# A new order of the work in each slot of an attention schedule, with another split of the PSUM banks

## Chip, cores and metric

The kernel runs on one core of one Trainium2 chip. The metric is device time in microseconds (us) of that core; "before" is the median of three runs.

## What is computed

One launch computes four residual layers over x, 8 batches of 256 × 512, all in fp32. The first two are attention, and they are what the change touches; the last two are scans over 256 time steps.

- Layer 0, masked attention: for each batch, q = xᵀ·Wqᵀ gives 512 tokens of 8 heads with 32 elements. Keys, queries and values are all q. Scores of masked keys are replaced by -1e30, rows of masked queries by zero; softmax, product with the values, output product with Wo, and x is added.
- Layer 1, modulated attention: RMS norm of x, scaled and shifted by a modulation that is computed from the condition (`emb @ W_emb + b_emb`); qkv product; RMS norm of q and k per head; softmax attention with 16 heads over 256 tokens; `o + o @ W_out`, and x is added.
- Layers 2 and 3: an oscillator integrated by four-stage Runge-Kutta steps and a GRU cell, both over 256 steps.

A softmax may be shifted by any number per query row; the kernel shifts by row maxima so that the exponentials stay in range.

## The kernel before

The engines are called PE (matmul), DVE (vector), ACT (scalar), POOL and SP (here the queue that issues every DMA). Each engine works through its own instructions strictly in program order, and the program order is written out by hand: `tc.manual_schedule()` with one loop over slots, g from -5 to 79 (lines 462 to 526). In each slot the loop calls one small step of several batches at once; a batch starts every U = 8 slots, so that a steady stretch repeats every eight slots (a "period"). The slots of a period are counted here as g mod 8, 0 to 7.

Layer 0 of a batch has two groups of four heads (e = 0, 1), each with four blocks of 128 keys (kc = 0 to 3), so eight blocks, one in each slot:

- `project` (line 170) makes q; DVE masks it into qm, ACT copies it; `project_out` (186) transposes the copy in the next slot.
- `scores0` (192): four matmuls, one for each head, into four PSUM banks, and four ACT copies into an SBUF block `sc`.
- `maxima0` (206): DVE's row maxima of a block, into `mxp0[e]`.
- `rows0` (212), once for each group, at the end of the slot of its fourth block: four PE transposes of `mxp0[e]`, an ACT copy, a DMA to DRAM (`row`) and a DMA that broadcasts the row to all partitions (`bc`, one buffer).
- `weights0` (224), five slots after the block's scores: DVE subtracts `bc` from the block, ACT exponentiates in place.
- `values0` (229), one slot later: eight matmuls, products with the values and with ones, accumulated over the four blocks in the banks c0 and c1. After the fourth, `weigh0` (246) divides on DVE and finishes on POOL.
- `masked_out` (260): output product and addition to x.

Layer 1 of a batch follows: `normalize` (273), `modulate` (285), six `qkv` products (300), one in each slot, with `qkv_norm` (323; DVE and POOL) and in the next slot `qkv_out` (337), which transposes q and k. Four head steps c = 0 to 3 then take one slot each:

- `maxima1` (346): sixteen matmuls into four banks, and four DVE maxima into `mxp1` (one buffer), which release the banks.
- one slot later `rows1` (362): transposes and an ACT copy `mrow`; `weights1` (369): scores again into four banks with the maxima subtracted by a matmul, and four ACT exponentials `ex`.
- one slot later `values1` (393): products into one more bank, `weigh` (162) on DVE.
- `modulated_out` (401) and, a slot later, `modulated_turn` (418), for each half of the tokens; its result goes out through SP (`x2d`).

For all but the last two batches a slot does one `qkv`; batches 6 and 7 do two. `modulation` (123) makes the scale and shift of all batches, once, in slot 4: 64 small matmuls, and the identity added to `wout_sb`.

[...] Everything but c0 and c1 takes its bank from one pool of six through `bank()` (lines 57 and 60). A tile that takes a bank over waits until the bank's last reader is done:

```python
ps_s = ctx.enter_context(tc.tile_pool(name="a_ps_s", bufs=6, space=PSUM))
ps_c = ctx.enter_context(tc.tile_pool(name="a_ps_c", bufs=1, space=PSUM))
...
def at(g, rel, n=1):
    b, r = divmod(g - rel, U)
    return (b, r) if 0 <= b < B and r < n else None
```

`at(g, -4, U)` names the block whose scores are made in slot g, `at(g, 1, U)` that of `weights0`, `at(g, 2, U)` that of `values0`. `heads(g, rel)` names the batch and head step in the same way.

Of the kernel before, what the change touches and what calls it, by code (L numbers as in the profile page):

```python
# [8 lines left out]
F32 = mybir.dt.float32  # L9
AF = mybir.ActivationFunctionType  # L10
ALU = mybir.AluOpType
AX = mybir.AxisListType
PSUM = bass.MemoryType.PSUM

P = 128
B, T, D = 8, 256, 512
NJ = D // P
# [7 lines left out]
def attention(ctx, tc, cst, x, cond, wqT, woT, w_emb, b_emb, g_norm, w_qkv, g_q, g_k, w_out, follow):  # L25
# [28 lines left out]
    first = ExitStack()  # L54
    fone = first.enter_context(tc.tile_pool(name="a_fone", bufs=1, side="right"))
    ftwo = first.enter_context(tc.tile_pool(name="a_ftwo", bufs=2, side="right"))
    ps_s = ctx.enter_context(tc.tile_pool(name="a_ps_s", bufs=6, space=PSUM))
    ps_c = ctx.enter_context(tc.tile_pool(name="a_ps_c", bufs=1, space=PSUM))

    def bank(shape, name):  # L60
        return ps_s.tile(shape, F32, tag="s", name=name)

    def line(name):
        return sm.tile([P, D], F32, tag="line", name=name, bufs=6)
# [14 lines left out]
    with tc.manual_schedule():  # L79
        nc.sync.dma_start(wq_sb, wqT.rearrange("(k p) e -> p k e", p=P))  # L80
        load(0)
        cst["rest"]()
        vec = wp.tile([12, P], F32, name="vec")
        nc.sync.dma_start(vec[0:8, :], b_emb.rearrange("(f p) -> f p", p=P))
        nc.sync.dma_start(vec[8:12, :], g_norm.rearrange("(f p) -> f p", p=P))
        gq_sb = wp.tile([P, 1], F32, name="gq_sb")
        gk_sb = wp.tile([P, 1], F32, name="gk_sb")
        for i in range(4):
            nc.sync.dma_start(gq_sb[32 * i : 32 * i + 32, :], g_q.unsqueeze(1))
            nc.sync.dma_start(gk_sb[32 * i : 32 * i + 32, :], g_k.unsqueeze(1))  # L90

        wemb = [
            two.tile([P, 2 * D], F32, tag=tag, name=f"wemb_{k}", bufs=bufs)
            for k, (tag, bufs) in enumerate((("qT", 1), ("kT", 1), ("vt", 2), ("vt", 2)))
        ]
        for k in range(NJ):
            nc.sync.dma_start(wemb[k], w_emb[k * P : (k + 1) * P, :])
        load(1)
        wo_sb = fone.tile([P, 2, 256], F32, name="wo_sb")
        nc.sync.dma_start(wo_sb, woT.rearrange("(k p) e -> p k e", p=P))  # L100
        wqkv_sb = wp.tile([P, NJ, 3 * D], F32, name="wqkv_sb")
        nc.sync.dma_start(wqkv_sb, w_qkv.rearrange("(k p) f -> p k f", p=P))
        wout_sb = wp.tile([P, NJ, D], F32, name="wout_sb")
        nc.sync.dma_start(wout_sb, w_out.rearrange("(k p) f -> p k f", p=P))

    gqs = wp.tile([P, 1], F32, name="gqs")
    mhalf = wp.tile([P, 16], F32, name="mhalf")
# [12 lines left out]
    vecT = wp.tile([P, 12], F32, name="vecT")  # L120
    ssT = wp.tile([P, 8, B], F32, name="ssT")

    def modulation():

        nc.vector.tensor_scalar_mul(gqs, gq_sb, SC)
        pv = bank([P, 28], "pvs")
        nc.tensor.transpose(pv, cst["vecs"], ident[0:28, 0:28])
        nc.vector.tensor_copy(cst["vecS"], pv)
        pv = bank([P, 12], "pv")
        nc.tensor.transpose(pv, vec, ident[0:12, 0:12])  # L130
        nc.vector.tensor_copy(vecT, pv)
        pe = bank([P, 8, B], "pe")
        for f in range(8):
            for k in range(NJ):
                nc.tensor.matmul(
                    pe[:, f, :],
                    lhsT=wemb[k][:, f * P : (f + 1) * P],
                    rhs=condT[:, k, :],
                    start=(k == 0),
                    stop=(k == NJ - 1),  # L140
                )
        nc.vector.tensor_tensor(ssT, pe, vecT[:, 0:8].unsqueeze(2).to_broadcast([P, 8, B]), ALU.add)
        nc.vector.tensor_scalar_add(G, ssT[:, 0:NJ, :], 1.0)
        nc.vector.tensor_tensor(G, G, vecT[:, 8:12].unsqueeze(2).to_broadcast([P, NJ, B]), ALU.mult)
        nc.vector.tensor_copy(shift, ssT[:, NJ:8, :])

        for c in range(NJ):
            nc.vector.tensor_add(wout_sb[:, c, c * P : (c + 1) * P], wout_sb[:, c, c * P : (c + 1) * P], ident)
# [75 lines left out]
    def weights0(b, e, kc):  # L224
        sc = scs[b, e, kc]
        nc.vector.tensor_sub(sc, sc, bcs[b, e])  # L226
        nc.scalar.activation(sc, sc, AF.Exp, bias=negT[:, kc, b : b + 1], scale=SC)  # L227

    def values0(b, e, kc):
        if kc == 0:  # L230
            if e == 0:
                ctxTs[b] = fone.tile([P, 2, D], F32, tag="ctxT", name=f"ctxT_{b}")
            pc0s[b, e] = [ps_c.tile([P, D], F32, tag=f"c{i}", name=f"pc0_{b}_{e}_{i}") for i in range(2)]
        sc = scs.pop((b, e, kc))
        for half in range(2):
            for h in range(4):
                o = e * P + h * DH
                nc.tensor.matmul(
                    pc0s[b, e][half][32 * h : 32 * h + 32, :],
                    lhsT=qtoks[b][:, kc, o : o + DH] if half == 0 else ones[:, 0:DH],  # L240
                    rhs=sc[:, h, :],
                    start=(kc == 0),
                    stop=(kc == NJ - 1),
                )
# [100 lines left out]

    def maxima1(b, c):
        qT, kT = qTs[b], kTs[b]
        ss = [bank([P, 2, 256], f"n1_{b}_{c}_{h}") for h in range(4)]
        for qc in range(2):
            for h in range(4):  # L350
                r = 32 * h
                nc.tensor.matmul(
                    ss[h][:, qc, :],
                    lhsT=qT[r : r + 32, c, qc * P : (qc + 1) * P],
                    rhs=kT[r : r + 32, c, :],
                    start=True,
                    stop=True,
                )
        for h in range(4):
            nc.vector.tensor_reduce(mxp1[:, :, 32 * h], ss[h], AX.X, ALU.max)  # L360
# [32 lines left out]
    def values1(b, c):  # L393
        if c == 0:
            oTs[b] = big.tile([P, NJ, 256], F32, tag="oT", name=f"oT_{b}")
        pc = bank([P, 2, 256], f"pc1_{b}_{c}")
        for half in range(2):
            values(pc, half, lambda k, h: vts[b][:, k, c * P + h * DH : c * P + (h + 1) * DH], [exs1[b, c]])
        weigh(pc, oTs[b][:, c, :], f"1_{b}_{c}")
# [44 lines left out]
    def at(g, rel, n=1):  # L444

        b, r = divmod(g - rel, U)
        return (b, r) if 0 <= b < B and r < n else None

    def heads(g, rel):

        for b in range(B):
            if 0 <= g - HEADS[b] - rel < NJ:
                return b, g - HEADS[b] - rel
        return None

    left = {}

    def leave(kind):
        for key in [k for k in left if k[0] == kind]:
            yield *key[1:], left.pop(key)  # L460

    with tc.manual_schedule():
        for g in range(-5, OUT[-1][1] + 2):

            if a := at(g, -4, U):
                scores0(a[0], a[1] // 4, a[1] % 4)
            if a := at(g, 2, U):
                values0(a[0], a[1] // 4, a[1] % 4)
            for a in leave("qt"):
                project_out(*a)  # L470
            if g == OUT[-1][1] + 1:
# [2 lines left out]
                modulated_turn(*a)  # L474
            if g - 1 in norms:
                modulate(norms.index(g - 1))
            if a := at(g, 1, U):
                weights0(a[0], a[1] // 4, a[1] % 4)
            if (a := at(g, 2, U)) and a[1] % 4 == 3:
                weigh0(a[0], a[1] // 4)  # L480

            if a := at(g, -5, 2):
                left["qt", a[0], a[1]] = project(*a)
            if a := at(g, U + 2):
                masked_out(a[0])
            if g == 4:
                modulation()
            if g in norms:
                normalize(norms.index(g))
            made = [(part, qkv(*part)) for part in parts.get(g, ())]  # L490
            for a in leave("qkv"):
                qkv_out(*a)
            for b in range(B):
                if g in OUT[b]:
                    m = OUT[b].index(g)
                    left["x2", b, m] = modulated_out(b, m)

            for part, lines in made:
                if lines:
                    qkv_norm(*part, *lines)  # L500
                    left["qkv", *part] = lines[1]
            if a := heads(g, 1):
                rows1(*a)
            a, a1 = at(g, -4, U), heads(g, 0)
            last = a and a[1] % 4 == 3
            if last:
                maxima0(a[0], a[1] // 4, 3)
            if a1:
                maxima1(*a1)
            if a2 := heads(g, 2):  # L510
                values1(*a2)
            if a2 := heads(g, 1):
                weights1(*a2)
            if a and not last:
                maxima0(a[0], a[1] // 4, a[1] % 4)
            if last:
                rows0(a[0], a[1] // 4)
            if (a2 := at(g, -7)) and a2[0] > 1:
                load(a2[0])
            if g == U * B + 2:  # L520
                first.close()
                follow()
                for (b, m), d in x2d.items():
                    nc.sync.dma_start(
                        cst["x2T"][:, :, b, m * P : (m + 1) * P], d.rearrange("p (j n) -> p j n", j=NJ)
                    )
# [486 lines left out]
```

## Time and profile before

| | us |
|---|---|
| median of three runs (2957.05 to 2961.34) | 2959.53 |
| the profiled execution, its own time | 2958.41 |
| its span, first to last instruction | 2956.6 |
| attention, to the last batch's last products | 876 |
| scans, the rest | 2080.6 |
| mean granted PE clock, share of full | 0.976 |

How to read it: the page's second part cuts the span into 40 slices, where each digit is a busy share in tenths and the row PEclk the granted clock in tenths. A stage row has the stage, its length, then busy us and instruction count of PE, of PE's weight loads (PEld), DVE, ACT and POOL, then granted clock, DMA share and GB/s. A row in order of time has start, length, engine, line, operation, what it writes and reads, its shape and count; what stands in brackets is the idle time before it and who ended it. Each fp32 matmul stands as two matmul records, so a block of four score matmuls is "x8". Groups that follow closely are merged, and a wait for a bank lies inside such a row, which then is longer than its work.

### The profile page before, as it was taken

The numbers are of one execution on the slowest core, as the hardware profiler recorded it, in microseconds if no ns is written. First come the engines' busy times: TensorE is split into PE (matmuls) and PEld (weight loads), VectorE is DVE, ScalarE is ACT, GpSimd is POOL, SyncE is SP. The second block draws the span as 40 slices with busy tenths as digits, with TensorE's granted clock in tenths as the row PEclk, the third lists the DMA queues.
The fourth block names the chain that finished last, engine by engine and source line by source line (L and its number), as shares of the span: only waits on it lengthen the run. The fifth ranks groups of instructions, "written<-read, shape, count | busy, mean of one in ns | idle before, by whom it ended". The sixth has DMA issues, their size and how long they took to land.

```text
span 2956.6 us, 159809 instructions
## 1 busy us (share of the span) xinstructions
PE 2720.4 (92%) x67258; PEld 1930.5 (65%) x67258; DVE 2124.6 (72%) x8948; ACT 1720.9 (58%) x8427; POOL 1049.1 (35%) x2945
## 2 busy tenths in 40 slices
PE   6789999999988999999999999999999999999997
PEld 3234444444546777777777777777777777777776
DVE  4866676666446777777777777777777777777773
ACT  4655566554335666666666666666666666666551
POOL 0233123312313444444444444444444444444442
PEclk7989999999999999999999999999999999999998
DMA  3110101000600000000000000000000000000000
GB/s 143 40 40 29 40 26 47 29 33 23 129 15 4 7 6 7 6 7 7 7 6 7 6 7 7 6 6 7 7 7 7 6 7 7 6 7 6 6 7 6
DMA packets 27559, 57.60 MB, mean 19 GB/s; under 512 B 2816, under 2 KB 17164, under 8 KB 24788
## 3 DMA queue, kind: packets, MB, share of 16 engines
q1 hardware_dynamic: 26836, 47.36, 5.3%
q8 instruction: 526, 8.62, 1.2%
q14 instruction: 197, 1.61, 0.2%
HBM read 40.15 MB, written 7.21 MB: 16 GB/s over the span
## 4 chain that ended last, share of the span: by engine, by line
PE 39%; DVE 24%; ACT 5%; issue 3%; ACTq 0%; POOL 0%; DVEq 0%; POOLq 0%
PE pg L744 19%; PE ic L709 18%; DVE icT L901 5%; DVE qn L902 5%; ACT tT L609 4%; DVE hqs L862 3%; DVE own L759 3%; DVE sqmm L858 2%; DVE v L761 2%; DVE hz L789 2%; DVE own L778 1%; ACT sqmm L847 1%; DVE own L784 1%; PE psx L405 1%; ACTq L609 0%
## 5 line engine op out<-in xcount | busy, mean ns | idle before, releaser
L709 PE MATMUL ic<-cT_sb,tT 128*8 128x128 f32 x32736 | 1086.1, 273 | 82.3 <-ACT tT L609 45.6
L709 PEld LDWEIGHTS ic<-cT_sb,tT 128*8 128x8 f32 x32736 | 760.1, 89 | 339.8 <-ACT tT L609 268.5
L744 PE MATMUL pg<-whh_sb,hz 128*32 128x128 f32 x24576 | 820.9, 275 | 49.4 <-DVE hz L789 17.6
L609 ACT ACTIVATE tT<-qn 128x16 f32<-128x16 f32 x2046 | 440.8, 216 | 636.9 <-DVE qn L902 516.4
L744 PEld LDWEIGHTS pg<-whh_sb,hz 128*32 128x32 f32 x24576 | 669.5, 110 | 123.1 <-DVE hz L789 122.9
L901 DVE STREAM_TRANSPOSE icT<-ic 128x64 f32<-128x64 f32 x2048 | 504.2, 246 | 67.6 <-PE ic L709 63.2
L902 DVE SCALAR_TENSOR_TENSOR qn<-icT,hqs 128x16 f32<-128x16 f32 x2048 | 350.7, 171 | 70.1
L704 POOL TENSOR_TENSOR W<-W,cx 128x128 f32<-128x128 f32 x765 | 297.3, 389 | 256.6 <-ACT cx L690 256.4
L697 POOL TENSOR_TENSOR W<-cx,us 128x128 f32<-128x128 f32 x255 | 116.9, 458 | 445.0 <-ACT cx L690 445.0
L858 DVE SCALAR_TENSOR_TENSOR sqmm<-sqmm,qn 128x32 f32<-128x32 f32 x768 | 153.5, 200 | 151.4 <-ACT sqmm L847 122.4
L862 DVE TENSOR_TENSOR hqs<-W,sqmm 128x32 f32<-128x32 f32 x1020 | 199.9, 196 | 46.1 <-DVE own L784 1.0
L723 PE MATMUL gi<-wih_sb,x3T 128*32 128x384 f32 (+2 forms) x3072 | 201.5, 379 | 0.5 <-POOL x3T L914 0.5
L690 ACT ACTIVATE cx<-qn 128x32 f32<-128x32 f32 x1280 | 200.9, 213 | 0.0
L227 ACT ACTIVATE sc<-sc,negT 128x2048 f32<-128x2048 f32 x64 | 128.6, 2010 | 89.2 <-DVE sc L226 79.2
L305 PE MATMUL psqkv<-wqkv_sb,xnT 128*128 128x512 f32 x384 | 174.8, 600 | 0.2 <-DVE oT L165 0.2
L690 ACT ACTIVATE cx<-p 128x32 f32<-128x32 f32 x1020 | 149.8, 217 | 32.4 <-DVE p L857 1.6
L226 DVE TENSOR_TENSOR sc<-sc,bc 128x2048 f32<-128x2048 f32 x64 | 147.8, 2310 | 11.9 <-DMA bc<-row 11.9
L203 ACT COPY sc<-s 128x512 f32<-128x512 f32 x256 | 132.1, 617 | 40.6 <-PE s L198 40.4
L759 DVE STREAM_TRANSPOSE own<-pg 128x128 f32<-128x128 f32 x256 | 84.8, 331 | 94.8 <-PE pg L744 94.8
L208 DVE TENSOR_REDUCE mxp<-sc 128x4 f32<-128x2048 f32 x64 | 145.8, 2279 | 6.7 <-ACT sc L203 6.7
L690 ACT ACTIVATE cx<-q 128x32 f32<-128x32 f32 x1020 | 145.5, 213 | 0.0
L847 ACT ACTIVATE sqmm<-qn 128x32 f32<-128x32 f32 x768 | 140.5, 183 | 0.6
(149 smaller groups left out, 3364.0 us busy)
## 6 DMA issues: line engine op xcount, KB each, us to landing
bc<-row SPq DMA_DIRECT2D x16, 1024.0 KB
x<-in_x SPq DMA_DIRECT2D x8, 512.0 KB
out<-o SPq DMA_DIRECT2D x256, 16.0 KB
wqkv_sb<-in_L_cond_W_qkv SPq DMA_DIRECT2D x1, 3072.0 KB
wih_sb<-in_L_cond_W_ih SPq DMA_DIRECT2D x4, 768.0 KB
whh_sb<-in_L_cond_W_hh SPq DMA_DIRECT2D x4, 768.0 KB
x2d<-x2o SPq DMA_DIRECT2D x11, 256.0 KB
x2T<-x2d SPq DMA_DIRECT2D x11, 256.0 KB
```

Of the source, the lines that this page charges most:

```text
L305: nc.tensor.matmul(ps, lhsT=xnTs[b][:, c, m * P : (m + 1) * P], rhs=wqkv_sb[:, c, part * D : (part + 1) * D], start=(c == 0), stop=(c == N ...
L609: nc.scalar.activation(tT, src[:, half * HM : (half + 1) * HM, :], AF.Tanh)
L690: nc.scalar.activation(c[:, i], x, AF.Copy, scale=f)
L704: nc.gpsimd.tensor_tensor(W[:, i + 1 : 5], W[:, i + 1 : 5], c, ALU.add)
L709: nc.tensor.matmul(ps[32 * j : 32 * j + B, :], lhsT=tT[k // HM][:, k % HM, :], rhs=cT_sb[:, k, j * P : (j + 1) * P], start=(k == 0), stop= ...
L723: nc.tensor.matmul(gi_ps[rows(j), g0:g1, :], lhsT=x3T[c][:, k, :], rhs=wih_sb[:, k, g0:g1, j * P : (j + 1) * P], start=(k == 0), stop=(k = ...
L744: nc.tensor.matmul(pg_ps[rows(j), :], lhsT=hzs[tau % 3][:, k, 32 * g : 32 * g + 32], rhs=whh_sb[:, k, g, j * P : (j + 1) * P], start=((k, ...
L759: nc.vector.transpose(pgt.rearrange("p m n -> p (m n)"), pg_ps)
L858: stt(mm, sq, LIN[s], qs, ALU.subtract, ALU.mult)
L862: nc.vector.tensor_sub(hq, W[:, s], mm)
L901: nc.vector.transpose(icT.rearrange("p m n -> p (m n)"), ic[:, half * 64 : half * 64 + 64])
L902: stt(qn[:, m2, :], icT[:, :, 0:B], IC[s], hq[:, m2, :], ALU.mult, ALU.add)
```

## The change

It is confined to the attention schedule.

1. PSUM: the common pool has five banks instead of six, and `values1` has a bank of its own, c2. For the last batch, two of the four banks of `maxima1` are c0 and c1.
2. Loads: `wqkv_sb` and `wout_sb` (3 MB and 1 MB) are issued at the end of slot -1, behind the first `rows0`, and no longer ahead of everything.
3. `modulation` runs in slots 3 to 6, a quarter each, with four small adds in place of one; the identity is added to `wout_sb` in slot 8.
4. `weights0` is cut in two: the subtraction stays, the exponential is `exps0`, which in the slots 3 to 7 of a period stands at the end of the slot, where `values0` now stands too; in the slots 0 to 2 both stay early.
5. For the batches 0 to 5, `maxima1` stands at the start of the slot in which its `rows1` and `weights1` stand, and the order of such a slot is `maxima1`, `values1`, `scores0`, `rows1`, `qkv`, `weights1`, `values0`. `weigh0`, where due there, moves into the next slot.
6. `rows0` is called near the start of a slot, for the group that `at(g, -5, U)` names.
7. `qkv_out` stands behind `modulated_out`; `rows1` near the middle of its slot.

```diff
-    ps_s = ctx.enter_context(tc.tile_pool(name="a_ps_s", bufs=6, space=PSUM))
+    ps_s = ctx.enter_context(tc.tile_pool(name="a_ps_s", bufs=5, space=PSUM))
...
+    def other_bank(shape, tag, name):
+
+        return ps_c.tile(shape, F32, tag=tag, name=name)
...
+    def load_weights():
+
         nc.sync.dma_start(wqkv_sb, w_qkv.rearrange("(k p) f -> p k f", p=P))
-        wout_sb = wp.tile([P, NJ, D], F32, name="wout_sb")
         nc.sync.dma_start(wout_sb, w_out.rearrange("(k p) f -> p k f", p=P))
...
-        pe = bank([P, 8, B], "pe")
-        for f in range(8):
+        pe = bank([P, 2, B], f"pe_{f}")
+        for i in range(2):
...
         nc.vector.tensor_sub(sc, sc, bcs[b, e])
+
+    def exps0(b, e, kc):
+        sc = scs[b, e, kc]
         nc.scalar.activation(sc, sc, AF.Exp, bias=negT[:, kc, b : b + 1], scale=SC)
...
-        ss = [bank([P, 2, 256], f"n1_{b}_{c}_{h}") for h in range(4)]
+
+        ss = []
+        for h in range(4):
+            n = f"n1_{b}_{c}_{h}"
+            ss.append(other_bank([P, 2, 256], f"c{h}", n) if b == B - 1 and h < 2 else bank([P, 2, 256], n))
...
-        pc = bank([P, 2, 256], f"pc1_{b}_{c}")
+        pc = other_bank([P, 2, 256], "c2", f"pc1_{b}_{c}")
...
+            a0, v0 = at(g, -4, U), at(g, 2, U)
+            w1, v1 = heads(g, 1), heads(g, 2)
+
+            a1, early = heads(g, 1, range(B - 2)), heads(g, 0, range(B - 2, B))
+            late = a1 is not None or heads(g, 0, range(B - 2)) is not None
+            turns = list(leave("qkv"))
+            if a1:
+                maxima1(*a1)
+                if v1:
+                    values1(*v1)
+                if a := due.pop("weigh", None):
+                    weigh0(*a)
+            elif a0:
+                scores0(a0[0], a0[1] // 4, a0[1] % 4)
+            if (a := at(g, -5, U)) and a[1] % 4 == 3 and g > 0 and not a1:
+                rows0(a[0], a[1] // 4)
+            if v0 and not late:
+                values0(v0[0], v0[1] // 4, v0[1] % 4)
...
+            if a1 and a0:
+                scores0(a0[0], a0[1] // 4, a0[1] % 4)
+            if (a := at(g, -5, U)) and a[1] % 4 == 3 and a1:
+                rows0(a[0], a[1] // 4)
+            if w1:
+                rows1(*w1)
+            if e0 := at(g, 1, U):
+                weights0(e0[0], e0[1] // 4, e0[1] % 4)
+                if not late:
+                    exps0(e0[0], e0[1] // 4, e0[1] % 4)
+            if v0 and not late and v0[1] % 4 == 3:
+                weigh0(v0[0], v0[1] // 4)
+            if a0 and a0[1] % 4 < 3:
+                maxima0(a0[0], a0[1] // 4, a0[1] % 4)
...
+            if 3 <= g < 7:
+                modulation(2 * g - 6)
+            if g == U:
+                add_identity()
...
+            if a0 and a0[1] % 4 == 3:
+                maxima0(a0[0], a0[1] // 4, 3)
+            if g == -1:
+                rows0(0, 0)
...
+            if not w1:
+                for a in turns:
+                    qkv_out(*a)
+            if early:
+                maxima1(*early)
+
+            if v1 and not a1:
+                values1(*v1)
+            if w1:
+                weights1(*w1)
+                for a in turns:
+                    qkv_out(*a)
+            if e0 and late:
+                exps0(e0[0], e0[1] // 4, e0[1] % 4)
+            if v0 and late:
+                values0(v0[0], v0[1] // 4, v0[1] % 4)
+                if v0[1] % 4 == 3:
+                    due["weigh"] = v0[0], v0[1] // 4
...
+            if g == -1:
+                load_weights()
```

## The prediction

> **What bounds the kernel now.** I read the page first, then the engines by stage, then the tensor engine (PE) in order of time. The page says PE busy 92% and puts the vector engine (DVE) second:
>
> ```profile
> PE 2720.4 (92%) x67258; PEld 1930.5 (65%) x67258; DVE 2124.6 (72%) x8948; ACT 1720.9 (58%) x8427; POOL 1049.1 (35%) x2945
> PEclk7989999999999999999999999999999999999998
> ```
>
> By stage, cut at the first matmul of each batch's masked output product (L265) and at the end of attention:
>
> ```profile
> 0.00:177.80 177.80, 129.40 (x663) 52.80 (x663) 115.07 (x86) 99.93 (x153) 31.03 (x32) 0.85 0.23 85
> 177.80:673.80 496.00, 466.46 (x3232) 212.94 (x3229) 341.96 (x290) 287.42 (x468) 129.62 (x112) 0.96 0.10 33
> 673.80:876.00 202.20, 185.93 (x1360) 95.95 (x1359) 97.14 (x109) 75.96 (x132) 51.36 (x40) 0.93 0.27 61
> 876.00:2956.60 2080.60, 1938.58 (x62011) 1568.78 (x62009) 1570.45 (x8465) 1257.62 (x7676) 837.13 (x2763) 1.00 0.03 7
> ```
>
> The last row, 2080.6 us of scans, has the same code in both kernels. Everything is decided in the first 876 us: 177.8 of start, five periods of 99 us, 202.2 of tail. The middle row looks full (466 of 496), but a matmul's row covers its wait for a bank. So I read spacing instead, start to start, in one period (475.9 to 574.9):
>
> ```profile
> 489.69 0.66 PE L340 MATMUL ptqk<-ident,qr 128*128 128x128 f32 x4 [1.49 <-POOL qr L330]
> ...
> 495.64 0.71 PE L352 MATMUL n<-kT,qT 32*128 32x256 f32 x8 [1.21 <-ACT qT L344]
> ...
> 507.04 0.77 PE L375 MATMUL s<-qT,kT 32*128 32x256 f32 x5 [1.14 <-ACT qt L182]
> ...
> 522.13 3.29 PE L198 MATMUL s<-qm 32*128 32x512 f32 x8
> 525.36 1.93 PE L238 MATMUL pc<-sc,qtok 128*32 128x512 f32 x8
> ...
> 536.70 2.51 PE L198 MATMUL s<-qm 32*128 32x512 f32 x8
> ...
> 550.51 1.62 PE L198 MATMUL s<-qm 32*128 32x512 f32 x8 [1.20 <-DVE oT L165]
> ```
>
> A score block takes 1.07 us where nothing holds it (483.29 to 484.36); here it takes 3.23 and 2.44, because four score banks wait for the four exponentials just before. Undisturbed spacings in this period: values0 1.86, qkv 3.43, masked_out 3.44, modulated_out 3.53, maxima1 1.07, values1 1.87, weights1 1.78, rows1 0.32, project 1.71, rows0 0.49. The sum: 8×(1.07+1.86) + 6×3.43 + 3.44 + 2×3.53 + 4×(1.07+1.87+1.78+0.32) + 2×1.71 + 5.8 for the small transposes = 84 us. So 15 of 99 us are lost. The granted clock of this period is 0.97: 0.03×99 = 3 us are half clock, 12 are waits.
>
> **Part by part.** *Load order.* The start hangs on one broadcast:
>
> ```profile
> 24.63 0.60 SPq L221 DMA_DIRECT2D row<-mrow  x1
> 32.99 0.35 SPq L222 DMA_DIRECT2D bc<-row  x1
> 37.72 2.29 DVE L226 TENSOR_TENSOR sc<-sc,bc 128x2048 f32<-128x2048 f32 x1 [7.33 <-DMA bc<-row]
> ```
>
> The 8 KB row needs 8.4 us because wqkv and wout (4 MB) were issued before it; the next row (54.63 to 56.39) needs 1.8. The loads now stand behind bc on SP's queue: bc at 26.4, subtraction at about 31, minus 6.6 to 7.3. The price: the second row queues behind the 4 MB; its reader is four slots away, and wqkv's first reader ten, so zero (about 5 us if that cover failed).
>
> *Modulation in four slots.* Today PE does its 64 matmuls in one piece and DVE starves:
>
> ```profile
> 70.00 0.22 DVE L142 TENSOR_TENSOR ssT<-pe,vecT 128x64 f32<-128x64 f32 x1 [9.83 <-PE pe L135]
> ```
>
> In the early slots DVE is the bound: subtraction 2.31 + maximum 2.28 each slot, weigh0 4.3 every fourth. Four pieces of some 2 us fit beside that; added are three adds of 0.22. I keep 2 us as still exposed: minus 8. The four identity adds (0.89) move to slot 8, behind a subtraction.
>
> *rows0.* The edit is named "next slot", but at(g,-5) is one slot earlier than at(g,-4). In the built order the transposes of a group stand behind its third score block, ahead of its third and fourth maxima, except the very first. They read older maxima for two of four query blocks: a different shift in those softmax rows. For time it means that PE no longer waits for a fresh maximum (2.65 at 53.66, about 3 at 121, 1.2 to 1.5 per period). bc then stands at the head of SP's queue for two slots, until the last subtraction with the old bc, instead of one; behind it are only the x2d writes, whose line buffers are wanted slots later: zero.
>
> *Slot order, banks.* The rotating pool has five banks, not six; values1 gets c2. In slots 4 to 7 of a period the order becomes maxima1, values1, scores0, rows1, qkv, weights1, values0: between weights1 and the next four-bank group stands values0 (1.86), which needs no pool bank, and between maxima1 and scores0 stands values1. I laid this order out with the measured durations (ex 0.52 per copy, sc 2.06 per four, exps0 2.01, n 2.49 per four, weigh 2.18). Waits left: slot 0 1.0 (values0 waits for exps0, now queued behind the four ex copies: 0.2+2.07+2.01 against 3.2 us of PE work); slot 2 1.4 (a score bank still holds modulated_out's product until DVE, behind weigh0 and a maximum, adds it); slot 3 0.8; slot 4 2.4 (ACT there has exps0, two copies, four xnT, four sc, mrow, qt, four ex: 10.5 us against 9.6 of PE); slots 5 and 6 0.9; slot 7 1.1 (DVE has 2.49+2.18+4.34+2.31+2.28 = 13.6 in slot 6 against 11.8 of PE, and its tail delays the next maxima). Sum 7.6 instead of 12. Q's output transposes move behind modulated_out, which removes the 1.49.
>
> [...]
>
> *Clock.*
>
> ```profile
> 305.00:312.00 7.00, 5.87 (x61) 3.86 (x59) 4.51 (x6) 5.19 (x10) 0.90 (x2) 1.00 0.48 170
> 312.00:319.00 7.00, 7.00 (x28) 2.44 (x26) 3.87 (x3) 3.35 (x7) 0.00 (x0) 0.51 0.01 2
> ```
>
> The clock column falls to 0.51 after a gap of 1.14 us at 308. [...]
>
> Period: 84+7.6+2 = 93.6 against 99, five times: minus 27. Start: 7 (load) + 8 (modulation) + 5 (rows0 waits up to 178) + 5 (bank waits and clock there) = minus 25. Tail: Q's transposes wait 3.4 at 687.6 and 3.7 at 829 today and cost clock behind them; rows0 waits 1.5; weights1 of slots 60, 61 and 66 takes 3 to 5 us too long each. Batches 6 and 7 keep maxima1 where it was, and their last slots are a chain that stays: minus 13 of some 20. Sum: 65. The profiled execution has 2958.41 (span 2956.6), so 2893; the median of the runs lies 1.1 above it: 2894.
>
> **Rivals.** (a) *Likeliest*, 2894, chance 0.52. (b) *The waits go nearly all*: period 86 with full clock, 13×5 + 25 + 18 = 108, 2851, chance 0.15. For: the small excess of each wait above; against: ACT's 10.5 us in slot 4 cannot be reordered away. (c) *New waits take the place in the middle*: period 98, start 22, tail 8: 35, 2924, chance 0.21. For: exps0 behind ex and weigh0 in slot 6 are new queues; against: DVE is busy only 69% in the middle. (d) *Slower*: DVE becomes the ring. maxima1's four reductions release the banks of scores0; if the subtraction and maximum of the slot before (4.6) stand ahead of them in all four head slots, a period pays 4×4.6 = 18 on 91, 109 us, and the five periods lose 50 against 38 gained elsewhere: about 2971, chance 0.08. It decides from 4 us per head slot on; my layout shows 1.1 in one slot. (e) Within 0.2%, the early gain eaten by (c) in full, 0.04. About 0.2% (6 us) is what a measurement here tells from no change.
>
> The range leaves out the outer half of (b), most of (d) and (e): 2853 to 2935. Faster 0.88, same 0.04, slower 0.08.
>
> **What would show it.** Right: bc issued within 2 us of its row near 25 us and the first subtraction at 31; no 9.8 us gap on DVE at 60 to 70; masked_out of batches 0 and 1 at about 91 and 152 instead of 109.7 and 177.8; five spacings of 93 to 94; score blocks behind weights1 at 1.1 to 1.5; the last row of the stage table unchanged. Wrong: spacing of 98 or more with gaps that end on ACT's exponentials (c), or reductions of maxima1 starting over 4 us late in each head slot (d).

## The result, and the profile after

The changed kernel takes 2912.4 us (median of four runs, 2911.4 to 2919.0) against 2960.4 of the kernel before beside it: a ratio of the means of 0.9845, 95% interval 0.9828 to 0.9862. The forecast was 2894 with a range of 2853 to 2935: the sign and the range held, but of the 65 us that were forecast 47 to 48 came. The profiled execution has a span of 2910.6 us, 46.0 below that of before. Executions of the kernel before differ by some 20 us, the shorter ones at the higher clock: of 44 further ones, 39 took 2953.8 to 2966.3 us at a mean granted clock of 0.973 to 0.978, and five 2934.3 to 2942.0 at 0.981 to 0.985. From the page of the changed kernel, the lines that answer to those of before:

```profile
PE 2705.6 (93%) x67258; PEld 1918.5 (66%) x67258; DVE 2126.1 (73%) x8951; ACT 1718.5 (59%) x8427; POOL 1098.7 (38%) x2945
PEclk8899999999999999999999999999999999999999
```

The same stages, cut at the first matmul of each batch's masked output product (now L281) and at the end of attention:

```profile
0.00:166.80 166.80, 132.69 (x666) 54.14 (x666) 118.22 (x90) 101.24 (x154) 34.57 (x33) 0.87 0.25 92
166.80:634.30 467.50, 454.10 (x3233) 203.85 (x3230) 343.43 (x291) 286.42 (x468) 172.55 (x112) 1.00 0.11 35
634.30:830.00 195.70, 180.72 (x1355) 91.88 (x1354) 93.13 (x107) 74.23 (x129) 54.46 (x39) 0.95 0.28 63
830.00:2910.60 2080.60, 1938.10 (x62013) 1568.64 (x62011) 1571.31 (x8465) 1256.58 (x7676) 837.08 (x2763) 1.00 0.03 7
```

The start went from 177.8 to 166.8 (minus 11.0, forecast 25), the five periods from 496.0 to 467.5 (minus 28.5, forecast 27), the tail from 202.2 to 195.7 (minus 6.5, forecast 13). The clock column of the middle is 1.00 and was 0.96. The products of batches 0 to 7 start at 103.1, 166.8, 260.9, 354.3, 447.6, 541.0, 634.3 and 723.8: the five periods are 93.3 to 94.1 long, as forecast, while the first two products were forecast for 91 and 152.

PE in order of time, one period (447.6 to 541.0), the score blocks that are held, and values0 behind one of them; a block takes 1.07 start to start where nothing holds it:

```profile
455.00 1.98 PE L211 MATMUL s<-qm 32*128 32x512 f32 x8
...
468.94 1.70 PE L211 MATMUL s<-qm 32*128 32x512 f32 x8
...
493.19 1.29 PE L211 MATMUL s<-qm 32*128 32x512 f32 x8
...
505.90 1.80 PE L211 MATMUL s<-qm 32*128 32x512 f32 x8
...
515.24 1.14 PE L211 MATMUL s<-qm 32*128 32x512 f32 x8
517.53 1.06 PE L254 MATMUL pc<-sc,qtok 128*32 128x512 f32 x8 [1.15 <-ACT sc L243]
...
535.74 2.35 PE L211 MATMUL s<-qm 32*128 32x512 f32 x8
```

No block behind heads waits 2.2 us any more. Two waits of a little over 1 us are left: values0 for exps0 at 517.5 (1.15), as the prediction laid out, and the block at 535.7 (1.2), of which more below. All others are under 0.9.

The start, SP's queue and DVE from the first row on:

```profile
27.87 0.60 SPq L234 DMA_DIRECT2D row<-mrow  x1
29.63 0.33 SPq L235 DMA_DIRECT2D bc<-row  x1
...
34.11 2.29 DVE L239 TENSOR_TENSOR sc<-sc,bc 128x2048 f32<-128x2048 f32 x1 [0.48 <-DMA bc<-row]
```

The row needs 1.8 us instead of 8.4, and DVE waits 0.48 instead of 7.33. The four adds of modulation wait 3.23 us at most, where one waited 9.83. Both edits shrank the waits they were aimed at, and the start still gained less than half of its sum. Here is where it stands still, in slot 9, the first slot of a new group (SP, DVE and PE mixed, in order of time):

```profile
84.35 0.33 SPq L235 DMA_DIRECT2D bc<-row  x1
...
89.88 2.29 DVE L239 TENSOR_TENSOR sc<-sc,bc 128x2048 f32<-128x2048 f32 x1 [2.56 <-DMA bc<-row]
92.09 1.75 DVE L271 RECIPROCAL r<-pc 128x256 f32<-128x256 f32 x1
...
96.33 2.28 DVE L221 TENSOR_REDUCE mxp<-sc 128x4 f32<-128x2048 f32 x1
...
98.67 0.90 PE L229 MATMUL pm<-ident,mxp 128*128 128x128 f32 x3 [9.01 <-DVE mxp L221]
99.50 1.94 PE L254 MATMUL pc<-sc,qtok 128*32 128x512 f32 x8
```

PE stands 9.01 us in front of rows0's transposes, which wait for the maximum of the slot before (L221 at 96.33). That maximum is queued on DVE behind weigh0 (92.09 to 96.4), which is queued behind the first subtraction, which waits for a broadcast that could be issued only at 84.35, after the last subtraction with the old bc. Up to 178 us PE waits 20.3 us in all for DVE's maxima in front of rows0's transposes; before it were 13.1. The prediction said "PE no longer waits for a fresh maximum" and counted 5 us for it.

### The profile page after: what moved, and what is told of

It reads as the page before. It is cut to its first block, busy times and chain, and to the rows that moved or that the text cites. A ratio compares the mean times of both kernels' runs of the same rounds, so it can differ in the third digit from the quotient of the medians.

```text
span 2910.6 us, 159805 instructions
## 1 busy us (share of the span) xinstructions
PE 2705.6 (93%) x67258; PEld 1918.5 (66%) x67258; DVE 2126.1 (73%) x8951; ACT 1718.5 (59%) x8427; POOL 1098.7 (38%) x2945
## 3 DMA queue, kind: packets, MB, share of 16 engines
q14 instruction: 197, 1.61, 0.2%
## 4 chain that ended last, share of the span: by engine, by line
PE 57%; DVE 29%; ACT 8%; issue 4%; POOL 1%; DMA 1%; ACTq 0%; SPq 0%; POOLq 0%; DVEq 0%
PE pg L795 19%; PE ic L760 18%; DVE icT L952 5%; PE psqkv L321 5%; DVE qn L953 5%; ACT tT L660 4%; DVE hqs L913 3%; PE pc L254 3%; DVE own L810 3%; DVE sqmm L909 2%; DVE v L812 2%; PE pc L167 2%; DVE hz L840 2%; PE s L211 2%; PE n L372 1%
## 5 line engine op out<-in xcount | busy, mean ns | idle before, releaser
L913 DVE TENSOR_TENSOR hqs<-W,sqmm 128x32 f32<-128x32 f32 x1020 | 199.9, 196 | 46.5 <-DVE own L835 1.1
L221 DVE TENSOR_REDUCE mxp<-sc 128x4 f32<-128x2048 f32 x64 | 145.9, 2282 | 39.9 <-ACT sc L216 39.9
L810 DVE STREAM_TRANSPOSE own<-pg 128x128 f32<-128x128 f32 x256 | 84.8, 331 | 91.8 <-PE pg L795 91.8
```

Source lines behind the costliest of these rows:

```text
L810: nc.vector.transpose(pgt.rearrange("p m n -> p (m n)"), pg_ps)
L913: nc.vector.tensor_sub(hq, W[:, s], mm)
```

## Theories and experiments

**Theory.** The start fell short because of rows0's place: PE's transposes stand ahead of values0 and wait for a maximum that stands behind weigh0. **Rivals**: the wait only covers another one (DVE's work, or the half clock, 40 to 41 us of the first 103 in both kernels); or load order and modulation are worth less than their gaps, because something else comes late next. For the middle the open point is whether the bank split is worth zero, as the prediction's sum has it, and for the tail why half was missing.

Times by stage come from one profiled execution each; start is up to batch 1's masked product, tail from batch 6's to the first matmul of the scans, and the last column is how long the clock stood at one half in the five periods (0.50 from 312.5 to 318.5 in the kernel before). The median of before is the one beside the changed kernel; beside the experiments it was 2957.7 to 2958.6.

| kernel | median | start | five periods | tail | half clock |
|---|---|---|---|---|---|
| before | 2960.4 | 177.8 | 496.0 | 207.5 | 41.0 |
| after | 2912.4 | 166.8 | 467.5 | 201.6 | 3.4 |
| r_slot3 | 2900.8 | 162.7 | 466.3 | 196.8 | 3.4 |
| r_next | 2912.0 | 163.4 | 469.9 | 205.4 | 10.2 |
| l_undo | 2916.3 | 171.0 | 467.5 | 202.8 | 3.4 |
| m_undo | 2915.6 | 169.1 | 467.5 | 202.8 | 3.4 |
| before_start | 2951.7 | 167.2 | 498.8 | 207.4 | 47.8 |
| n_max | 2896.0 | 156.4 | 465.2 | 199.9 | 0 |
| weigh_first | 2931.3 | 174.8 | 479.9 | 196.8 | 21.5 |
| b_undo | 2897.3 | 167.0 | 459.3 | 192.3 | 3.4 |
| before_bank | 3014.8 | 177.2 | 546.1 | 213.1 | 105.8 |
| t_rows1 | 2905.0 | 163.0 | 467.6 | 195.4 | 3.4 |
| best | 2916.5 | 170.2 | 478.8 | 191.1 | 24.8 |
| best2 | 2885.4 | 156.6 | 458.4 | 190.5 | 6.8 |

One row is a warning: t_rows1 has the changed kernel's code up to batch 6, and its start is 3.8 us shorter. So a start of a single profile is known to some 4 us. The five periods took 467.5 to 467.6 us in all four profiles that share their code (after, l_undo, m_undo, t_rows1), and the tail 201.6 to 202.8 in the three that share it.

### rows0 one slot later (r_slot3)

```diff
-            if (a := at(g, -5, U)) and a[1] % 4 == 3 and g > 0 and not a1:
+            if (a := at(g, -4, U)) and a[1] % 4 == 3 and g > 0 and not a1:
...
-            if (a := at(g, -5, U)) and a[1] % 4 == 3 and a1:
+            if (a := at(g, -4, U)) and a[1] % 4 == 3 and a1:
```

> Edit: the changed kernel with rows0 one slot later (slots 3 and 7 of a period instead of 2 and 6): behind the third maximum of its group, still ahead of the fourth, so that one of four query blocks is shifted by an older maximum. Theory A (the start fell short of its forecast because the four transposes of rows0 stand on PE ahead of values0 and wait for the maximum of the slot before, which DVE makes only after weigh0, 4.3 us): in slot 3 that maximum is a slot old and the weigh0 lies behind, so the 42 us of PE waits on DVE's maxima before 178 us shrink to under 15; first masked output product at 93 to 97 instead of 103.1, second at 155 to 159 instead of 166.8, total 2900 to 2904. Theory B (DVE's work and the half clock bound the start; the wait only covers another one): first product no earlier than 100, total 2909 or more.

The total is theory A's, 2900.8 (ratio to the kernel before 0.9817, 0.9785 to 0.9848), 11.6 below the changed kernel. Its place is not: the first product came at 97.9 and the second at 162.7, 4 to 5 us earlier and not 8 to 12, which is hardly more than two profiles of one code differ by, and 4.8 us came from the tail. Yet rows0's wait is gone. The row of waits of its transposes up to 180 us, in the changed kernel:

```profile
  DVE mxp L221: 42.0, 14
```

and in this one:

```profile
  DVE mxp L221: 4.4, 3
```

This view counts a wait twice, in front of the matmul and in front of its weight load. PE's own share is 20.3 us in the changed kernel and 1.8 here (the "42 us of PE waits" of the expectation was the double count). So 18.5 us of waiting were taken away and about 4 us of time. The rest of the wait has only changed its name; slot 9 again, in this kernel:

```profile
87.65 2.29 DVE L239 TENSOR_TENSOR sc<-sc,bc 128x2048 f32<-128x2048 f32 x1 [2.72 <-DMA bc<-row]
89.86 1.75 DVE L271 RECIPROCAL r<-pc 128x256 f32<-128x256 f32 x1
...
94.33 1.94 PE L254 MATMUL pc<-sc,qtok 128*32 128x512 f32 x8 [7.58 <-DVE ctxT L272]
```

values0 of the new group needs the banks c0 and c1, which weigh0 reads to 94.2. The chain old bc, broadcast, first subtraction, weigh0 is the same; only the maximum behind it (2.3 us) and the transposes have left it. The sum says the same: all idle gaps of PE from 23.5 us to batch 1's product are 27.9 us in the changed kernel and 23.3 here. In the kernel before they were 40.8: 16.4 of values0 for exponentials, 11.9 of values0 for weigh0, 11.2 of rows0. In the changed kernel, where rows0 stands ahead of values0, 20.3 of the 27.9 are rows0's and 1.7 those of values0 for exponentials. Theory A holds for the sum, theory B for where the wait goes.

### rows0 after the fourth maximum (r_next)

```diff
-            if (a := at(g, -5, U)) and a[1] % 4 == 3 and g > 0 and not a1:
+            if (a := at(g, -3, U)) and a[1] % 4 == 3 and g > 0 and not a1:
...
-            if (a := at(g, -5, U)) and a[1] % 4 == 3 and a1:
+            if (a := at(g, -3, U)) and a[1] % 4 == 3 and a1:
```

> Edit: the changed kernel with rows0 two slots later (slots 0 and 4), in the slot after that of its fourth block, so that all four query blocks are shifted by their own maxima; the very first rows0 stays. Theory A: the wait for the fourth maximum is as long as for the one of any slot before (its DVE work is subtraction 2.3 and maximum 2.3), but no weigh0 stands ahead of it; and bc is wanted one slot later, so row, broadcast and their 4 us may be exposed on DVE: 2902 to 2912 in all, with gaps of DVE that end on bc of 1 to 3 us per group. Theory B: within 3 us of the changed kernel if bc is in time, and slower (2915 to 2930) if bc is exposed in each of 16 groups.

2912.0 (2904.0 to 2915.8), at the upper edge of theory A's span but also where theory B put an unexposed bc: it doesn't tell them apart. The first product is at 99.3; DVE's waits for bc up to 640 us grow from 4.8 us (3) to 10.8 us (6), about 2 us each as theory A said. So the place that the change's name tells of, with every query block shifted by its own maxima, costs no more time than the one it has.

### The loads ahead again (l_undo), modulation in one piece (m_undo)

```diff
+    with tc.manual_schedule():
+        load_weights()
...
-            if g == -1:
-                load_weights()
```

> Edit: the changed kernel with the 4 MB of wqkv and wout issued ahead of everything, as before. Theory A (the first subtraction waits for the row's broadcast, and all that follows is shifted by it): the row takes 8 us again, first subtraction some 6 us later, total plus 5 to 8, 2917 to 2920. Theory B (the start is bound by PE waits and half clock further on, which swallow the delay): first subtraction later, second batch's masked product within 2 us of 166.8, total 2911 to 2914.

The median is 3.9 us higher and the start 4.2 later: between the theories, and of 7 forecast. The runs overlap (2910.7 to 2918.8 against 2911.4 to 2919.0), and one start is known to 4 us, so the size is not settled. In this kernel the row is issued at 27.25 and bc at 33.16; in the kernel before it was 24.63 and 32.99. The broadcast is let go at 33 either way, however late the row is: the 4 MB end then (in the kernel before the DMA share is 1.04 from 30 to 31 us, 0.63 in the next and 0.07 from 32 to 33). So the edit is worth the time from the row to 33, and in every kernel run here but the one before the first row is issued at 26.7 to 28.4, as its first blocks run later. DVE waits 4.57 us for bc, and its first subtraction is at 37.58 against 34.11, 3.5 us. Why the early slots are later than in that one profile stays open. It is not the order of the loads: before_bank, further down, keeps the old one and issues its row at 27.46 and bc at 33.20.

```diff
-            if 3 <= g < 7:
-                modulation(2 * g - 6)
-            if g == U:
+            if g == 4:
+                for f in range(0, 8, 2):
+                    modulation(f)
                 add_identity()
```

> Edit: the changed kernel with all four quarters of modulation (and the identity adds right behind them no longer in slot 8 but there) in slot 4. Theory A (DVE starves behind PE's 64 matmuls, and DVE sets the pace there): one DVE gap of 8 to 10 us in slot 4 again, total plus 6 to 9, 2918 to 2921. Theory B (PE sets the pace of the start, by its wait for maxima, and the same 64 matmuls cost it the same time wherever they stand): plus 0 to 3.

The median is 3.2 us higher and the start 2.3 later: theory B, or nearly, and again not told from nothing (2910.3 to 2917.8). DVE's gaps at the four adds are 0.17, 1.61, 1.89 and 3.24 us, 6.9 in all; in the changed kernel two are left, of 1.18 and 3.23. So in the new order the edit takes 2.5 us of DVE's gaps away, not 8, and the start's 2.3 fit that. PE's waits for rows0's maximum are 20.3 us in both, so they were not what gave way.

### Both alone, on the kernel before (before_start)

The edit is the second and third of the change's list alone, on the old slot order, old rows0 and old banks.

> Edit: the kernel before with the load order and modulation in four slots alone (the identity in slot 8); slot order, rows0 and banks as before. Theory A (in the old order both hit DVE while it sets the pace, as the prediction had it: 7 + 8): first masked output product at 94 to 98 instead of 109.7, total 2943 to 2947. Theory B (they are worth what undoing them in the changed kernel cost, 4 + 2, because PE's waits for rows0's maximum lie over both): first product at 103 to 105, total 2953 to 2956.

2951.7, 6 below the kernel before beside it, with a ratio of the means of 0.9988 (0.9971 to 1.0006): the total is not told from no change. The start is, with 167.2: minus 10.6, while the five periods took 2.8 longer with more half clock. It lies between the theories (first product 99.4). DVE's wait for the first bc is 0.69 here, and its gaps at the adds are 2.9 in all, so 13.5 us of gaps went, and most of them were time. That is nearly the whole of the changed kernel's 11.0; so all other parts together, the slot order, rows0 and the banks, brought the start 0.4 us, within the 4 that a profile is known to, where 10 were forecast for them.

### DVE's work in the start (n_max)

Beside rows0's place of r_slot3, the maxima of batch 1 are left out:

```diff
-            if a0 and a0[1] % 4 < 3:
+            if a0 and a0[1] % 4 < 3 and a0[0] != 1:
...
-            if a0 and a0[1] % 4 == 3:
+            if a0 and a0[1] % 4 == 3 and a0[0] != 1:
```

> Edit: rows0 in slots 3 and 7 (the best of the runs so far), and the eight maxima of batch 1 in layer 0 left out (its shift is that of batch 0): 8 x 2.28 us less on DVE, six of them ahead of the first masked output product. Nothing on PE changes. Theory A (with rows0's wait gone, DVE's work is what bounds the start: it stands still for 4 us only between 60 and 98): first product at 86 to 91 instead of 97.9, second at 147 to 154 instead of 162.7, total 2887 to 2894. Theory B (half clock and PE's own order bound it): first product at 95 to 98, total 2897 to 2901.

Against r_slot3, 13.7 us less on DVE bring the first product 3.2 us forward (94.7, just below theory B's span), 18.2 us bring the second 6.3 us (156.4); the total falls by 4.8 (2892.5 to 2898.5 against 2899.2 to 2901.6), to just below theory B's. By these starts a quarter to a third of the work taken away came back as time, so DVE's quantity of work is only a part of the bound. The next run tries the order across a change of groups.

### weigh0 ahead of the subtraction (weigh_first)

Again beside rows0's place of r_slot3:

```diff
+            if v0 and not late and v0[1] % 4 == 3:
+                weigh0(v0[0], v0[1] // 4)
             if e0 := at(g, 1, U):
                 weights0(e0[0], e0[1] // 4, e0[1] % 4)
...
-            if v0 and not late and v0[1] % 4 == 3:
-                weigh0(v0[0], v0[1] // 4)
```

> Edit: rows0 in slots 3 and 7, and in slots 1 and 5 (where no head step runs) weigh0 ahead of the subtraction on DVE, no longer behind it. Theory A (the start is a chain across the change of groups: last subtraction with the old bc, broadcast of the new one, first subtraction, weigh0, and only then are c0 and c1 free for PE's next values0; one such wait on PE is 7.6 us at 94.3): weigh0 runs while the broadcast is under way, that wait shrinks to 3 to 5 us, first masked output product at 93 to 95.5 instead of 97.9, total 2893 to 2899. Theory B (the wait is only moved: the exponential and the values behind the later first subtraction end when they ended): first product within 1 us of 97.9, total 2899 to 2903.

Both theories missed: 2931.3, 30 us above r_slot3. Slot 9 in this kernel:

```profile
88.53 1.76 DVE L271 RECIPROCAL r<-pc 128x256 f32<-128x256 f32 x1 [0.85 <-PE pc L254]
...
92.78 2.28 DVE L239 TENSOR_TENSOR sc<-sc,bc 128x2048 f32<-128x2048 f32 x1
...
97.16 1.93 PE L254 MATMUL pc<-sc,qtok 128*32 128x512 f32 x8 [7.62 <-ACT sc L243]
```

weigh0 does run while the broadcast is under way, and the banks are free at 92.9. But the subtraction now comes at 92.78 instead of 87.65, ACT's exponential behind it ends at 97.1, and values0 needs that too. There are two branches to the same matmul, subtraction then exponential (4.3 us) and weigh0 (4.3 us), and whichever DVE does second is late by the other. In the steady stretch it costs too: weigh0 waits on DVE for values0 (0.71 us at 640.1) with a ready subtraction behind it, a stretch of half clock of 3.4 us comes back in most periods, and a period is 95.8 instead of 93.1.

### The banks (b_undo, before_bank)

```diff
-    ps_s = ctx.enter_context(tc.tile_pool(name="a_ps_s", bufs=5, space=PSUM))
+    ps_s = ctx.enter_context(tc.tile_pool(name="a_ps_s", bufs=6, space=PSUM))
...
-        pc = other_bank([P, 2, 256], "c2", f"pc1_{b}_{c}")
+        pc = bank([P, 2, 256], f"pc1_{b}_{c}")
```

> Edit: the changed kernel with the PSUM split undone: a pool of six banks again, values1 from the pool, no c2. Theory A (the sum of the prediction: a copy more or less behind a four-bank group lies under values0 or values1, so the split costs and brings nothing by itself): 2909 to 2916, period 93 to 94. [...] Theory C (c2 brings something: with values1 in the pool, its bank is held until DVE's weigh and the next four-bank group waits for it): the period grows to 95 to 98, 2922 to 2935.

2897.3, 15.1 below the changed kernel: the split costs, so theory A's zero and theory C fall. An estimate from the measured copy, 0.52 us more for each of the 16 four-bank groups of a period, would be 8 us a period; with a period of 91.8 against 93.3 it is far less. PE in order of time shows the place. Slot 2 of a period with six banks:

```profile
526.37 3.60 PE L425 MATMUL psx<-wout_sb,oT 128*128 128x512 f32 x8
530.33 1.14 PE L211 MATMUL s<-qm 32*128 32x512 f32 x8
531.56 0.65 PE L229 MATMUL pm<-ident,mxp 128*128 128x128 f32 x4
```

The block is followed after 1.23 us; in the changed kernel, 535.74 to 538.02, after 2.28. There modulated_out's product still occupies one of five banks, until DVE has added it to x; neither values nor heads stand in front of the block to cover that, and the block's last weight load waits for it:

```profile
536.97 0.29 PEld L211 LDWEIGHTS s<-qm 32*128 32x128 f32 x2 [0.92 <-DVE x L430]
```

Slot 3 pays 0.84 at its block (455.00) and gets it back in the next product. Slot 4 pays the rest: modulated_turn's transposes stand right behind maxima1's four banks, and have to wait for its first maximum:

```profile
467.16 0.66 PE L441 MATMUL ptx<-ident,x 128*128 128x128 f32 x4 [0.18 <-DVE mxp L380]
```

With six banks that wait is gone, and the `project` a few rows further on starts 0.53 earlier in its period; from there to slot 2 the two kernels are alike within 0.1 us. So the price of the split is 1.05 us in slot 2 and 0.53 in slot 4, 1.6 of a period of 93.3, 8 in the five, and another 9 in the tail of this profile; the medians differ by 15 in all.

The other way round, on the old order:

```diff
-    ps_s = ctx.enter_context(tc.tile_pool(name="a_ps_s", bufs=6, space=PSUM))
+    ps_s = ctx.enter_context(tc.tile_pool(name="a_ps_s", bufs=5, space=PSUM))
...
-        pc = bank([P, 2, 256], f"pc1_{b}_{c}")
+        pc = ps_c.tile([P, 2, 256], F32, tag="c2", name=f"pc1_{b}_{c}")
```

> Edit: the kernel before with the PSUM split alone (pool of five, values1 in c2), all else as it was. Theory A (split worth nothing by itself): within 5 us of the kernel before, period 98 to 100. [...] Theory C (c2 brings something in any order): period 95 to 97, 2940 to 2950.

3014.8, a ratio of 1.0202 (1.0175 to 1.0228): theory A's 5 us and theory C's gain both fall. By stage, batch 1's to batch 6's product:

```profile
177.20:723.30 546.10, 525.24 (x3232) 243.09 (x3229) 342.38 (x290) 287.49 (x468) 129.59 (x112) 0.90 0.08 30
```

A period is 109.2 instead of 99.0. Of these 10 us the half clock has about 6, by an estimate: it holds for 105.8 instead of 41.0 us of the five periods, and of the 65 us more about half, 32, is lost. The rest, some 4, is left for longer waits with one bank less; which blocks pay it was not taken apart. So the same split costs 10 us a period in the old order and 1.6 in the new one.

### The tail (t_rows1), and all together (best, best2)

```diff
-            if w1:
+            if a1:
                 rows1(*w1)
...
+            if w1 and not a1:
+                rows1(*w1)
             if not w1:
                 for a in turns:
```

> Edit: the changed kernel, with rows1 of the last two batches at its old place, behind the slot's qkv and modulated_out, instead of ahead of them. Theory A (the tail gained 6.5 us and not 13 because the new place makes PE wait for a maximum of the slot just before, 1.9 us at 723.5 and 2.2 at 788.8, and the modulated_out behind each runs at half clock, 5.3 instead of 3.5 us): both waits go and most of the half clock with them: total minus 4 to minus 8, 2904 to 2909. Theory B (the transposes only wait for the same maximum later, in front of weights1, as the last head steps are a chain through DVE): 2910 to 2914.

2905.0 (2902.1 to 2912.9), 7.4 below the changed kernel, whose runs it just overlaps, and the tail 6.2 shorter, which is well beyond the 1.2 by which tails of one code differ: theory A, with theory B's wait in it. The changed kernel's tail, PE in order of time:

```profile
723.55 0.44 PE L385 MATMUL pm<-ident,mxp 128*128 128x128 f32 x2 [1.58 <-DVE mxp L380]
...
735.10 5.34 PE L425 MATMUL psx<-wout_sb,oT 128*128 128x512 f32 x8
```

and in t_rows1:

```profile
721.70 0.38 PE L385 MATMUL pm<-ident,mxp 128*128 128x128 f32 x2
...
726.17 0.49 PE L395 MATMUL s<-qT,kT 32*128 32x256 f32 x3 [1.33 <-ACT mrow L387]
...
730.12 4.14 PE L425 MATMUL psx<-wout_sb,oT 128*128 128x512 f32 x8
```

The transposes no longer wait; 1.33 us return at weights1, which needs what they make; but modulated_out takes 4.14 us instead of 5.34, as 1.1 us of it and not 3.5 fall into half clock. In the second such place the wait of 1.97 us (at 788.8) is gone too, and modulated_out takes 3.60 us instead of 5.29.

best is r_slot3, b_undo, t_rows1 and weigh_first in one.

> Edit: the changed kernel with everything together that should help: rows0 in slots 3 and 7, the pool of six banks with values1 from it, rows1 of the last two batches at its old place, weigh0 ahead of the subtraction in slots 1 and 5. If the parts add (12 for rows0, 15 for the banks, 4 to 8 for rows1, 2 to 6 for weigh0): 2871 to 2879. If they share the same waits (the tail's half clock above all, which rows0, the banks and rows1 all claim): 2882 to 2890, and the period stands at 91.5 in either case.

2916.5: weigh_first spoils it as it spoiled r_slot3 (period 95.3, not 91.5). best2 leaves it out.

> Edit: the changed kernel with rows0 in slots 3 and 7, the pool of six banks with values1 from it, and rows1 of the last two batches at its old place; weigh0 stays behind the subtraction. If the three parts add as they measured one by one (11.6, 15 and 7.4 us below the changed kernel): 2878, first masked output product at 98, period 91.5. If they share the tail's half clock, of which each claimed some 5 us: 2884 to 2892, with the same first product and period and only the tail short of the sum.

2885.4 (2884.9 to 2886.1), a ratio to the kernel before of 0.9752 (0.9738 to 0.9765): 27 us faster than the changed kernel and the fastest of all. The period is 91.4. The parts don't add to 34; the tail gains 11.1 us, where the three alone had gained 4.8, 9.3 and 6.2 of it. That is the second reading: they share the tail's half clock. It holds for 20.5 us of the changed kernel's tail, for 10.2, 6.8 and 13.6 in r_slot3, b_undo and t_rows1, and for 10.2 in best2. Half of it counted as lost, the parts claim 15.4 us and together save 5.1; the difference of 10 is about the 9.2 that are missing.

## Why the prediction was right in sign and short in size

- *Load order, minus 7.* The wait at the first subtraction fell from 7.33 to 0.48 as forecast. What it was worth is some 4 (l_undo: a wait of 4.57 for bc, the start 4.2 later, the totals not told apart): a row behind the 4 MB lands at 33 us, and with the row issued at 27.9 instead of 24.6 there was less to save. The first subtraction stands at 34.11 and not at 31. The cover claimed for the second row held: issued at 40.94 behind the 4 MB, it is there when the bc buffer comes free at 54.3.
- *Modulation, minus 8.* The gap of 9.83 became gaps of 1.18 and 3.23, where the step kept 2. Undone in the new order the gaps are only 2.5 us longer, and the start is 2.3 later (m_undo). In the old order both edits together have 10.6 of the forecast 15.
- *rows0's waits up to 178 us, minus 5.* This is the step that failed. The sentence "PE no longer waits for a fresh maximum" holds in the steady period (0.63 for the four transposes at 494.4, 0.59 at 538.0). It is false in the start, because the maximum that the new place reads last is that of the slot just before, and in slots 2 and 6 that slot holds weigh0: PE's waits grew from 13.1 to 20.3 us. And most of such a wait is no time that can be had: removed (18.5 us less in r_slot3), some 14 of it came back as other waits, above all for c0 and c1.
- *Bank waits and clock of the start, minus 5.* No run shows any: 0.4 us for all parts but the edits of loads and modulation, rows0's longer waits among them, and with the split undone the start is the same (167.0). What the slot order alone brought there stays open.
- *Five periods, minus 27.* Measured 28.5. That the number fits is luck: its two halves were wrong in opposite directions. The half clock of the kernel before held for 41.0 us in five periods, so by an estimate 4.1 us of each were lost to it, and nearly all of that came back; the prediction put 3. The 2 us that its period of 93.6 still has for it are a term that no run of the changed kernel shows: in its place 3.4 us of half clock are left in five periods, 0.3 us of each by the same estimate. So the clock gave 3.8 us a period and not 1. The waits, 99 less 84 less 4.1, were 10.9 and are 9.0 (93.3 less 84 less 0.3): they fell by 1.9 and not by 4.4. Without the split (b_undo) the rest of the change takes the five periods from 496.0 to 459.3, and the split gives 8 back; which step of the slot order brings how much of the 37 no run separates. No score block stands right behind weights1 any more; those behind values1 take 1.07, 1.22 and 1.74 against the forecast 1.1 to 1.5.
- *The split at zero.* The sum has no term for it; it costs 1.6 us a period and 15 in all. Of the 8 a period that the estimate of one copy more for each four-bank group gives, the new order covers all places but two, the block of slot 2 and the transposes of slot 4. The wait of 1.4 in slot 2 stands in the prediction's list, put down to modulated_out; 1.05 of the 1.2 measured there go when the sixth bank comes back. (The 2.4 of slot 4 in that list is more than its own numbers, 10.5 against 9.6 us, give.)
- *Tail, minus 13.* Measured 6.5 (5.9 to the scans' first matmul). The waits of Q's transposes shrank (3.40 to 1.86 at 649.2, and none is left of the one near the end, 3.44 in the trace and 3.7 in the prediction); what the sum left out is rows1's new place in the last two batches, where its maximum is fresh: 6 us by t_rows1, and the split, another 9 of this part by b_undo, some of them the same.
- *Rivals.* (b), (d) and (e) did not happen. (c), 12 us off, is nearer in the total than (a), 18 off, but not for its reason: its period of 98 was 93.3. The time lies between (a) and (c), because the start and the tail, not the middle, took the gain.

## What to carry over

A wait in front of an engine is worth its time only if nothing else holds the next instruction (in r_slot3 18.5 us of waiting went, and about 4 us of time): before a sum is made from a wait, write down what the instruction behind it needs as well, and when that comes. A step that is moved to an earlier slot reads what the slot before made last, so look at what stands ahead of that on its maker's queue, in the irregular slots as well as in the steady ones. A buffer or a bank that costs 1.6 us a period in one order can cost 10 in another, so try the two parts of such a change apart. And before waits are added up, look whether the view counts one wait on two engines.

## What the hardware showed

- In the five periods of the kernel before the clock stands at one half in nine stretches: seven of 3.41 to 3.42 us, one of 6.83 and one of 10.24. The changed kernel has one there, of 3.41 us, at 182. In the old order with five banks (before_bank) one period has three, of 6.83, 10.24 and 3.41 us, while the longest interval between two matmuls of that period is under 2 us. What starts such a stretch is not shown: the kernel before has one at 312.1, after its wait of 1.14 us at 308, while the changed kernel has a wait of 1.15 us at 517 and keeps its full clock (1.00 from 515 to 522).
- Periods of 93.3, 99.0 and 109.2 us go with 3.4, 41.0 and 105.8 us of half clock in five of them. By the estimate that half of it is lost, 3.8 of the 5.7 us by which a period shrank are clock, and 6.5 of the 10.2 by which it grew with five banks in the old order; what is left for the waits themselves is about a third of either.
- A reader that waits for bc starts 4.5 to 5.5 us after its issue in the changed kernel (29.63 to 34.11, 84.35 to 89.88). With one bc buffer that time stands open where DVE has nothing else to do at a change of groups: 4.8 us of DVE's waits in three places up to 640 us.
